# A macaron network on one core: feed-forward, norm and keys of three chunks inside the mixture of experts ahead of them, constant rows in two halves, transfers issued by SP

## The chip, the core and the metric

The kernel runs on one core of a Trainium2 chip. A core has five engines that run at the same time, each through its own instruction stream in order: PE (matrix products into PSUM), DVE (elementwise work and reductions), ACT (activation functions and copies), POOL (GpSimd), and SP, which here only issues transfers between HBM and the on-chip memory SBUF. An engine waits for another through semaphores. The metric is the device time of one execution in microseconds: 4069.91 us before the change, the median of three runs (4068.77 to 4074.88).

## What is computed

The input x has 2048 rows of 128 numbers. Blocks are added to it one after another; each reads a layer norm of x:

```python
x = x + 0.5 * L0_ffn(ln(x)); x = x + L0_attn(ln(x)); x = x + 0.5 * L0_ffn(ln(x))
x = x + 0.5 * L1_ffn(ln(x))        # first mixture of gated experts
x = x + L1_attn(ln(x))             # a long convolution
x = x + 0.5 * L1_ffn(ln(x))        # second mixture of gated experts
x = x + 0.5 * L2_ffn(ln(x))        # silu(x Wg) * (x Wu), then Wd; 384 hidden
x = x + L2_attn(ln(x))             # 16 heads of 8, rotary positions, no mask
x = x + 0.5 * L2_ffn(ln(x)); x = x + 0.5 * L3_ffn(ln(x))
x = x + L3_attn(ln(x))             # 16 heads, rotary, causal
x = x + 0.5 * L3_ffn(ln(x))
```

L1_ffn scores 8 experts for each row, keeps the two best with softmax weights, and adds the experts' outputs, each `(silu(x W1) * (x W2)) W3`. L3_ffn is a gated attention of 16 heads followed by a sparse mixture of 8 experts. Everything is in 32-bit floats, and a 32-bit product takes two passes on PE, which the trace lists as two matmuls.

## The kernel before

**Tiles.** x stays in SBUF as 16 tiles of 128 rows, and four of these (512 rows) make a chunk; there are four chunks, 0 to 3. A chunk is transposed (xnT, 128x512) to be the operand of products.

**The mixtures (`l1_ffn`, L526).** The norms of all four chunks are made first (`normed`), with the gate's logits (pl) and the choice of two experts (`top2`). Then a loop over chunks and experts makes, in two halves hb, two products h of 512 columns, Silu of the first on ACT (L554) and the product of both on DVE (L555, `hid`), and then 16 matmuls po with W3; four DVE operations (L563) add po, times the gate, to x. Every PE matmul goes through `mm`, whose line is L75, and every DVE operation of the helper `vec` has line L83. PSUM has eight banks: two for norms and logits, two each for the two h and for po.

**Order.** The kernel is written for a framework whose scheduler places the instructions of each engine by an estimate of when their inputs are ready, earlier text first. Instructions that are "pinned" keep the order of the text on their engine: on PE where `order["pinned"]` is set, on DVE, for `vec`, in the modes "core" and "drain". The mode names the phase: "free" outside the attentions, "fill" at an attention's beginning until its first product for weights, "core", and "drain" once all its scores are made.

**Between the second mixture and the first attention.** `head_buffers` (L1408) makes the tiles kp (keys of all heads), qps (four query tiles) and va (values). Each head's rows of kp and qp stand beside constant rows of zeros and ones, which are copied from a table `rest` in HBM (L1416, L1421) by SP. kp lies in memory that the mixtures' weights hold until then. After that, for chunks 0, 1, 2: `l2_chunk` (norm, transposes xn_tp, products gu with Wg and Wu, Silu, po with Wd, x updated) and `rope2.prepare` (norm again, transposes, keys: products pj, two DVE operations with the tables cos and sin, a sum on POOL, a rounded part hi on ACT and the rest lo on POOL). `send` writes hi and lo to HBM (dk for keys, dq for queries, L694), and `load_keys` brings the keys back to kp in the order of heads (L713): eight transfers a chunk in two halves of heads, of which an attention's first units need the first. Chunk 0 makes its queries too. Chunk 3 is carried into the attention as a guest.

**The attention (`attend`, L856).** A unit is a chunk of queries and a group of four heads. Scores (sn, L886) go to a maximum per row on DVE (h_mx); a unit's maxima become rows of its query tile; LAG (four) steps after, its weights (st, then Exp on ACT, pr) and outputs (av) begin. The first unit takes its keys chunk by chunk. Beside each step two guests advance by a stage: the carried chunk 3, and values and further queries. `begin` (L865) loads a unit's queries from dq into a query tile (L871). There are four attentions: L2 (rope2), gated, L3 (rope3), gated. Before the third the sparse experts run, and rope3 makes chunks 0 to 2 in "free" mode as each chunk's output is ready.

**The norm (`norm`, L177).** Statistics by bn_stats and bn_aggr, then `inv_sqrt` (L161): an estimate from integer operations and three Newton rounds, all small DVE operations of 128x4, and then one scaling for each tile, on ACT with `on_act`, else on DVE. `put` and `evac` copy PSUM to SBUF, ACT and DVE in turn except in "fill" (ACT) and "drain" (DVE). `queue` gives SP and ACT in turn in "free" and "fill", else SP.

Of the kernel before, what the change touches and what calls it, by code (L numbers as in the profile page):

```python
# [21 lines left out]
P = 128  # L22
# [20 lines left out]
def tile_macaron(ctx: ExitStack, tc: tile.TileContext, a: dict, out: bass.AP):  # L43
# [34 lines left out]
    class Ordered:  # L78
        def __getattr__(self, name):
            method = getattr(nc.vector, name)  # L80

            def call(*args, **kw):
                ins = method(*args, **kw)  # L83
                if order["mode"] in ("core", "drain"):
                    tc.keep_in_program_order(ins)
                return ins

            return call
# [3 lines left out]
    def transpose(dst, src):  # L92
        pin(nc.tensor.transpose(dst, src, ident))  # L93

# [66 lines left out]
    def inv_sqrt(pool, var, shape, tag):  # L161
# [3 lines left out]
        vec.tensor_single_scalar(g, v.bitcast(I32), 1, op=ALU.logical_shift_right)  # L165
        vec.tensor_scalar(g, g, -1.0, float(0x5F3759DF), ALU.mult, ALU.add)
        r = pool.tile(shape, F32, tag=tag + "_r", name=tag + "_r")
        prev = g.bitcast(F32)
        for _ in range(3):
            h = pool.tile(shape, F32, tag=tag + "_h", name=tag + "_h")  # L170
            vec.tensor_tensor(h, prev, prev, ALU.mult)
            vec.scalar_tensor_tensor(h, h, -0.5, v, ALU.mult, ALU.mult)
            vec.scalar_tensor_tensor(r, h, 1.5, prev, ALU.add, ALU.mult)
# [3 lines left out]
    def norm(src, dst, on_act=False):  # L177
# [5 lines left out]
        rstd = inv_sqrt(small, mv[:, :, 1], [P, TC], "ln")  # L183
        if on_act:
            nb = small.tile([P, TC], F32, tag="ln_nb", name="ln_nb")
            vec.scalar_tensor_tensor(nb, mv[:, :, 0], -1.0, rstd, ALU.mult, ALU.mult)
# [339 lines left out]
    def l1_ffn(w):  # L526
        HB = 2
        with ExitStack() as es:
            sb1 = es.enter_context(tc.tile_pool(name="m1", bufs=1))
            sb = es.enter_context(tc.tile_pool(name="m", bufs=3))  # L530
            psum = es.enter_context(tc.tile_pool(name="m_ps", bufs=2, space=PSUM))
            _, xnT = normed(psum)
            pl = psum.tile([P, NT, E], F32, tag="tp", name="pl")
            for i in range(NT):
                mm(pl[:, i, :], xnT[:, i * P : (i + 1) * P], w["l1_gT"])
            logits = sb1.tile([P, NT, E], F32, name="logits")
            nc.vector.tensor_copy(logits, pl)
# [6 lines left out]
            nc.vector.tensor_scalar_mul(gate, gate, 0.5)  # L544
            for c in range(NC):
                xc = xnT[:, c * CW : (c + 1) * CW]
                for e in range(E):
                    hid = sb.tile([P, HB, CW], F32, tag="hid", name="hid")
                    for hb in range(HB):
                        p_1 = psum.tile([P, CW], F32, tag="h1", name="h1")  # L550
                        p_2 = psum.tile([P, CW], F32, tag="h2", name="h2")
                        mm(p_1, w["l1_w12T"][:, e, hb * P : (hb + 1) * P], xc)
                        mm(p_2, w["l1_w12T"][:, e, (HB + hb) * P : (HB + hb + 1) * P], xc)
                        nc.scalar.activation(hid[:, hb, :], p_1, AF.Silu)  # L554
                        nc.vector.tensor_tensor(hid[:, hb, :], hid[:, hb, :], p_2, ALU.mult)  # L555
                    po = psum.tile([P, TC, D], F32, tag="po", name="po")
                    for t in range(TC):
                        for hb in range(HB):
                            mm(po[:, t, :], hid[:, hb, t * P : (t + 1) * P], w["l1_w3T"][:, e, hb, :],
                               start=hb == 0, stop=hb == HB - 1)  # L560
                    for t in range(TC):
                        i = c * TC + t
                        nc.vector.scalar_tensor_tensor(  # L563
                            x[:, i, :], po[:, t, :], gate[:, i, e : e + 1], x[:, i, :], ALU.mult, ALU.add
                        )
# [15 lines left out]
    pools = {}  # L581

    def ring(name, tag="w", shape=(P, CW), bufs=10):
        return pools["ring"].tile(list(shape), F32, tag=tag, name=name, bufs=bufs)
# [3 lines left out]

    def banks(name):
        return pools["sc"].tile([P, 2, CW], F32, tag="sc", name=name)  # L590
# [9 lines left out]
    def put(dst, src):  # L600
        if order["mode"] == "drain":
            vec.tensor_copy(dst, src)
        elif order["mode"] == "fill":
            nc.scalar.copy(dst, src)
        else:
            evac(dst, src)

    def queue():
        turn["q"] += 1
        return nc.scalar if order["mode"] in ("free", "fill") and turn["q"] % 2 else nc.sync  # L610
# [23 lines left out]
    def l2_chunk(c, w):  # L634
# [5 lines left out]
        for hb in range(HB):  # L640
# [4 lines left out]
            if order["mode"] == "free":  # L645
# [22 lines left out]
    class Heads:  # L668
# [38 lines left out]
        def load_keys(self, c, halves=(0, 1)):  # L707
# [9 lines left out]
            if 0 in halves:  # L717
                self.loaded.add(c)
# [137 lines left out]
    def attend(A, carried, follow, after=None):  # L856
# [4 lines left out]
        for c, halves in A.waiting_keys:  # L861
            A.load_keys(c, halves)
# [132 lines left out]
        if units[0] not in queries:  # L995
            begin(A, units[0])
        LAG = 4
# [8 lines left out]
        while nw < len(weights) or last:  # L1006
# [12 lines left out]
            if s and s[3] not in B.loaded:  # L1019
# [388 lines left out]
    def head_buffers(pool):  # L1408
# [4 lines left out]
        for j in range(2):  # L1413
            r = slice(j * KD + 4 * HD, (j + 1) * KD)
            for c in range(NC):
                nc.sync.dma_start(  # L1416
                    out=kp[r, :, c * CW : (c + 1) * CW].bitcast(F32),
                    in_=rest[0:n, :].unsqueeze(1).to_broadcast([n, NH // 2, CW]),
                )
            for qp in qps:  # L1420
                nc.sync.dma_start(  # L1421
                    out=qp[r, :, :].bitcast(F32), in_=rest[2 : n + 2, :].unsqueeze(1).to_broadcast([n, 2, CW])
# [150 lines left out]
```

## Time and profile before

| | value |
|---|---|
| median of three runs | 4069.91 us |
| the profiled execution: its time | 4074.4 us |
| the profiled execution: its span | 4072.6 us |
| PE matmuls, busy | 3557.4 us (87%), 29080 matmuls |
| DVE, busy | 3141.5 us (77%), 5645 instructions |
| ACT, busy | 2329.1 us (57%), 4436 instructions |
| POOL, busy | 215.0 us (5%), 262 instructions |
| mean granted clock of PE | 0.885 |

The profile records when each instruction of each engine began and ended, from the span's start. The page cuts the span into 40 slices of about 102 us; a digit is the busy share in tenths, and PEclk is the clock that PE was granted:

```profile
PE   8789898689999995899999965599997899999965
DVE  3855443579999975899999745689997799999844
ACT  1222122158888862688888722246675488888732
PEclk8889798779999997899999966668998799999966
```

Counted from 0, slices 2 to 3 and 4 to 6 hold the two mixtures, and the runs of nines from slice 8 on are the attentions. Slice 7 (713 to 814 us) lies ahead of the first attention, and slices 23 to 25 hold the sparse experts and what leads to the third. In a timeline line the columns are start, duration, engine, source line, operation, output<-inputs, shapes and count, and in brackets the idle time before it and what ended that; SPq and ACTq are transfers that SP and ACT issue.

### The profile page before, as it was taken

What the parts mean: (1) busy time and instruction counts of PE and PEld (TensorE: products, weight loads), DVE (VectorE), ACT (ScalarE), POOL (GpSimd) and SP (SyncE); (2) the same over time, 40 slices, a digit from 0 to 9 for tenths busy, and PEclk for the clock granted to TensorE, in tenths of its full rate; (3) what the DMA queues carried; (4) which work ended last, traced back from release to release, by engine and by line L of the source; (5) the groups of instructions that cost most, each with busy time, mean ns of one, the idle gap of its engine ahead of it and who ended that gap; (6) DMA issues with size and microseconds to landing.
All of it is one profiled execution on the core that took longest, in us unless ns stands there. A gap on an engine that the chain in (4) does not pass through costs nothing. (4 is left out here: it accounts for less than half of the span.)

```text
span 4072.6 us, 72035 instructions
## 1 busy us (share of the span) xinstructions
PE 3557.4 (87%) x29080; PEld 1680.4 (41%) x29080; DVE 3141.5 (77%) x5645; ACT 2329.1 (57%) x4436; POOL 215.0 (5%) x262
## 2 busy tenths in 40 slices
PE   8789898689999995899999965599997899999965
PEld 8566664333333342333333343243333333333334
DVE  3855443579999975899999745689997799999844
ACT  1222122158888862688888722246675488888732
POOL 2000000100000000000000033100000000000013
PEclk8889798779999997899999966668998799999966
DMA  2100003220000002100000022400002200000012
GB/s 71 25 1 1 1 1 87 62 63 7 10 7 10 4 13 57 50 9 9 7 10 4 9 70 77 110 20 10 10 2 62 54 10 7 10 7 7 7 42 74
DMA packets 71532, 111.91 MB, mean 27 GB/s; under 512 B 9712, under 2 KB 29920, under 8 KB 70944
## 3 DMA queue, kind: packets, MB, share of 16 engines
q1 hardware_dynamic: 57536, 77.81, 7.2%
q0 software_dynamic: 7088, 20.81, 2.1%
q10 hardware_dynamic: 6576, 8.69, 0.8%
q8 instruction: 229, 3.75, 0.4%
q14 instruction: 103, 0.84, 0.1%
HBM read 74.47 MB, written 31.75 MB: 26 GB/s over the span
## 5 line engine op out<-in xcount | busy, mean ns | idle before, releaser
L83 DVE TENSOR_REDUCE h_mx<-sn 128x2 f32<-128x1024 f32 (+1 forms) x1856 | 2206.3, 1197 | 141.4 <-PE sn L886 119.8
L942 ACT ACTIVATE pr<-st 128x512 f32<-128x512 f32 x3712 | 1972.7, 585 | 518.7 <-PE st L75 335.7
L75 PE MATMUL av<-pr,va 128*32 128x256 f32 x14592 | 1191.4, 399 | 10.9 <-ACT h_ot L971 10.9
L75 PE MATMUL st<-qp,kp 64*128 64x512 f32 x3712 | 998.4, 500 | 49.2 <-ACT pr L942 45.6
L886 PE MATMUL sn<-kp,qp 64*128 64x512 f32 (+3 forms) x3712 | 812.1, 416 | 126.6 <-DMA qp<-dq 46.1
L75 PEld LDWEIGHTS st<-qp,kp 64*128 64x128 f32 x3712 | 394.4, 188 | 818.1 <-ACT pr L942 441.8
L75 PEld LDWEIGHTS av<-pr,va 128*32 128x32 f32 x14592 | 293.1, 109 | 664.7 <-issue 626.8
L886 PEld LDWEIGHTS sn<-kp,qp 64*128 64x128 f32 x3712 | 388.7, 195 | 186.6 <-issue 99.8
L75 PE MATMUL h<-xnT,w_l_w12T 128*128 128x512 f32 x512 | 250.1, 611 | 1.7 <-DVE xnT L65 1.7
L554 ACT ACTIVATE hid<-h 128x512 f32<-128x512 f32 x128 | 76.4, 597 | 301.4 <-PE h L75 301.4
L75 PEld LDWEIGHTS po<-w_l_w3T,hid 128*128 128x128 f32 x1024 | 131.2, 193 | 69.1 <-DVE hid L555 47.2
L563 DVE SCALAR_TENSOR_TENSOR x<-po,gate,x 128x128 f32<-128x128 f32 x256 | 71.9, 344 | 100.4 <-PE po L75 100.3
L75 PE MATMUL po<-w_l_w3T,hid 128*128 128x128 f32 x1024 | 139.9, 279 | 1.3 <-DVE hid L555 1.3
L555 DVE TENSOR_TENSOR hid<-hid,h 128x512 f32<-128x512 f32 x128 | 87.2, 683 | 55.1 <-PE h L75 55.1
L75 PEld LDWEIGHTS h<-xnT,w_l_w12T 128*128 128x128 f32 x512 | 90.2, 197 | 66.1 <-issue 62.6
L1270 POOL DMA_INDIRECT wt<-in_b_wt,w_row_i x30 | 28.8, 960 | 1436.6 <-DVE slot_i L83 1395.0
L915 ACT CAST h_mT<-mt_ps 8x512 fp32r<-8x512 f32 x64 | 36.9, 576 | 100.4 <-PE mt_ps L93 100.2
L83 DVE BATCH_NORM_STATS2 st<-ph 128x6 f32<-128x256 f32 x46 | 19.9, 432 | 87.0 <-PE ph L75 87.0
L223 POOL TENSOR_TENSOR x<-x,w_b_n2b 128x512 f32<-128x512 f32 x8 | 10.1, 1266 | 1301.1 <-DVE rows L83 1133.7
L93 PE MATMUL xn_tp<-ident,xn_t 128*128 128x128 f32 x64 | 20.1, 406 | 66.3 <-ACT xn_t L189 62.7
L83 DVE TENSOR_TENSOR sn<-sn,mask_qk 128x256 f32<-128x256 f32 x128 | 54.2, 426 | 30.7 <-PE sn L886 29.3
L83 DVE TENSOR_TENSOR st<-st,mask_kq 128x128 f32<-128x128 f32 x256 | 63.3, 291 | 14.0 <-PE st L75 13.4
(391 smaller groups left out, 2627.5 us busy)
## 6 DMA issues: line engine op xcount, KB each, us to landing
qp<-dq SPq DMA_DIRECT2D x128, 136.0 KB
kp<-dk SPq DMA_DIRECT2D x128, 128.0 KB
dq<-hi SPq DMA_DIRECT2D x23, 256.0 KB
dq<-lo SPq DMA_DIRECT2D x23, 256.0 KB
wt<-in_b_wt SPq DMA_DIRECT2D x16, 258.0 KB
kp<-rest SPq DMA_DIRECT2D x8, 512.0 KB
dk<-lo SPq DMA_DIRECT2D x16, 256.0 KB
qp<-h_mT SPq DMA_DIRECT2D x256, 4.0 KB
```

Source lines behind the costliest of these rows:

```text
L75: pin(nc.tensor.matmul(dst, lhsT=lhsT, rhs=rhs, start=start, stop=stop))
L83: ins = method(*args, **kw)
L93: pin(nc.tensor.transpose(dst, src, ident))
L223: nc.gpsimd.tensor_tensor(xs, xs, row.unsqueeze(1).to_broadcast([P, TC, D]), ALU.add)
L554: nc.scalar.activation(hid[:, hb, :], p_1, AF.Silu)
L555: nc.vector.tensor_tensor(hid[:, hb, :], hid[:, hb, :], p_2, ALU.mult)
L563: nc.vector.scalar_tensor_tensor(x[:, i, :], po[:, t, :], gate[:, i, e : e + 1], x[:, i, :], ALU.mult, ALU.add)
L886: pin(nc.tensor.matmul(sc[:, j, :wd], lhsT=qp[r, p, t * P : (t + 1) * P], rhs=kp[r, 2 * g + p, kc * CW : kc * CW + wd], start=True, stop=True,
L915: nc.scalar.copy(mT, pt)
L942: nc.scalar.activation(pr[:, off:CW], sc[:, off:], AF.Exp, scale=A.scale)
L1270: nc.gpsimd.indirect_dma_start(wts[k], None, a["b3_wt"], bass.IndirectOffsetOnAxis(ap=w_row_i[:, s - E : s - E + 1], axis=0),)
```

## The change

1. `l1_ffn` takes a list of tasks. Its norms and logits get a PSUM pool of their own, closed before the pool of h and po opens. The expert loop is written out in two stages: `first` (h, Silu, product) yields after each half hb, and `second` (po, and the update of x) of the expert before follows after the first half of the next. For the second mixture the tasks are `l2_chunk` and `rope2.prepare` of chunks 0, 1 and 2. Chunk c's task begins when the last expert has updated chunk c, and a stage of it is written after each half of the experts of chunk c+1. There the mode is "host": PE and DVE are pinned, po has one bank, and three banks serve the guests, which so take gu in two separate banks. Chunk 3 stays a guest of the attention.
2. In "host" and "fill" a norm with its scaling on ACT makes its Newton rounds on POOL (12 operations and two for the offset in place of ten of DVE). For all norms the integer estimate takes one operation in place of two.
3. The constant rows come in two halves: those of the first query tile and the first half of heads in `head_buffers`, the others inside `attend` of rope2. `attend` now calls `begin` for its first unit ahead of the keys, and loads all chunks' first halves, then the other rows, then second halves; a score waits only for the half that it reads.
4. `put` uses ACT in every mode but "drain", and `queue` always gives SP. xnT moves to a pool that lasts, and the pools of the L2 and L3 weights open earlier.

The diff, cut to its core ("..." stands for lines left out):

```diff
     def inv_sqrt(pool, var, shape, tag, on_pool=False):
...
-        vec.tensor_single_scalar(g, v.bitcast(I32), 1, op=ALU.logical_shift_right)
-        vec.tensor_scalar(g, g, -1.0, float(0x5F3759DF), ALU.mult, ALU.add)
+        vec.tensor_scalar(g, v.bitcast(I32), -0.5, float(0x5F3759DF), ALU.mult, ALU.add)
...
+            if on_pool:
+                nc.gpsimd.tensor_tensor(h, prev, prev, ALU.mult)
+                nc.gpsimd.tensor_tensor(h, h, v, ALU.mult)
+                nc.gpsimd.tensor_scalar(h, h, -0.5, 1.5, ALU.mult, ALU.add)
+                nc.gpsimd.tensor_tensor(r, h, prev, ALU.mult)
...
+        on_pool = on_act and order["mode"] in ("host", "fill")
...
+    def l1_ffn(w, tasks=()):
...
+            with tc.tile_pool(name="m_pre", bufs=2, space=PSUM) as psum:
+                _, xnT = normed(psum)
...
+            psum = es.enter_context(tc.tile_pool(name="m_ps", bufs=2, space=PSUM))
+            if tasks:
+                pools["ring"] = es.enter_context(tc.tile_pool(name="early", bufs=1))
+                pools["tp"] = es.enter_context(tc.tile_pool(name="early_ps", bufs=3, space=PSUM))
+                order["pinned"], order["mode"] = True, "host"
...
             for c in range(NC):
                 for e in range(E):
+                    for hid in first(c, e):
+                        if late:
+                            second(*late)
+                            if late[1] == E - 1 and tasks:
+                                waiting.append([n, tasks.pop(0)])
+                            late = None
+                        if waiting and waiting[0][0] <= n:
+                            later = next(waiting[0][1], None)
+                            if later is None:
+                                waiting.pop(0)
+                            else:
+                                waiting[0][0] = n + later
+                        n += 1
+                    late = (c, e, hid)
+            second(*late)
...
     def banks(name):
+        if order["mode"] == "host":
+            return TwoBanks(name)
...
     def queue():
-        turn["q"] += 1
-        return nc.scalar if order["mode"] in ("free", "fill") and turn["q"] % 2 else nc.sync
+        return nc.sync
...
         A.current = True
-        for c, halves in A.waiting_keys:
-            A.load_keys(c, halves)
...
         if units[0] not in queries:
             begin(A, units[0])
+        for h in range(2):
+            for c, halves in A.waiting_keys:
+                if h in halves:
+                    A.load_keys(c, (h,))
+            if h == 0 and A is rope2:
+                other_rows()
...
-            if s and s[3] not in B.loaded:
+            if s and (s[3], s[1][1] // 2) not in B.loaded:
...
+        constant_rows(qps[0:1], slice(0, 4))
         nc.gpsimd.memset(va_flat, 1.0)
-        return kp, va_flat, qps
+        return kp, va_flat, qps, lambda: constant_rows(qps[1:], slice(4, 8))
...
-            l1_ffn(w1)
+            rope2, rope3 = RopeHeads("l2", w2, False), RopeHeads("l3", w3, True)
+            l1_ffn(w1, [chain([l2_chunk(c, w2), rope2.prepare(c)]) for c in range(NC - 1)])
...
-    for c in range(NC - 1):
-        finish_all([l2_chunk(c, w2), rope2.prepare(c)])
```

## The prediction

> **What bounds the kernel now.** I read first how busy each engine is by stage (windows), then the order of time around the seams, then the waits of SP. The columns of the first view are the stretch, its length, and busy time with count for PE, weight loads, DVE, ACT and POOL, then the granted clock, the DMA share and GB/s.
>
> ```profile
> 496.00:664.00 168.00, 167.37 (x759) 103.61 (x758) 82.55 (x227) 39.79 (x65) 0.00 (x0) 0.98 0.00 1
> 664.00:750.00 86.00, 52.62 (x159) 27.80 (x157) 31.60 (x152) 19.87 (x43) 13.83 (x10) 0.76 0.59 135
> 750.00:821.00 71.00, 37.74 (x121) 18.82 (x120) 39.55 (x59) 5.85 (x11) 8.44 (x9) 0.69 0.26 67
> 821.00:851.00 30.00, 23.17 (x44) 8.12 (x44) 19.50 (x22) 3.00 (x4) 7.12 (x8) 0.50 0.46 124
> 851.00:1500.00 649.00, 640.02 (x5993) 244.82 (x5992) 616.36 (x631) 546.49 (x1014) 2.52 (x2) 0.99 0.03 9
> 2548.00:2574.00 26.00, 0.44 (x1) 0.28 (x1) 4.69 (x16) 2.26 (x5) 4.89 (x5) 0.50 0.67 144
> ```
>
> The second mixture (496 to 664) and the attention (851 on) are full on PE. Between them lie 187 us in which no engine is, at a clock of 0.5 to 0.76: chunks 0 to 2 one after another, then chunk 3 beside the first scores. A second hole, at 2548, is before the third attention. The order of time says what ends each:
>
> ```profile
> 658.81 2.74 PE L75 MATMUL h<-xnT,w_l_w12T 128*128 128x512 f32 x6
> 659.01 1.13 DVE L563 SCALAR_TENSOR_TENSOR x<-po,gate,x 128x128 f32<-128x128 f32 x4 [1.92 <-PE po L75]
> 664.37 1.80 SPq L1416 DMA_DIRECT2D kp<-rest  x4
> 685.44 2.42 ACT L189 ACTIVATE xn_t<-x,ln_nb,ln_r 128x128 f32<-128x128 f32 x6 [8.19 <-DVE ln_nb L83]
> 692.64 0.75 DVE L83 SCALAR_TENSOR_TENSOR rot<-pj,w_l_bcol,cos 128x512 f32<-128x512 f32 x1 [5.97 <-DMA cos<-in_l_cos]
> 750.03 0.50 PE L886 MATMUL sn<-kp,qp 64*128 64x512 f32 x2
> 821.19 0.76 PE L886 MATMUL sn<-kp,qp 64*128 64x512 f32 x1 [12.88 <-DMA kp<-dk]
> ...
> 2552.37 15.29 SPq L713 DMA_DIRECT2D kp<-dk  x19
> 2568.21 11.34 SPq L871 DMA_DIRECT2D qp<-dq  x8
> 2573.51 0.44 PE L886 MATMUL sn<-kp,qp 64*128 64x128 f32 x1 [28.16 <-DMA qp<-dq]
> ```
>
> Constant rows (5 MB) start when the mixture's last matmul frees the memory, and hold up the tables; the first score is at 750, the fourth key chunk's at 821, the first product for weights at 851.13. At 2573 the first score waits 28 us for queries whose load stands on SP behind 19 key loads.
>
> **The guests, in PE work.** A chunk has 12 matmuls gu and 4 pj of 512 columns (0.428 us each at full clock, from six h in 2.74), 24 po (0.107 each, from 14 in 1.76) and 8 transposes (some 0.13): 6.85 + 2.57 + 1.0 = 10.4. Three chunks and the four pj of chunk 0's queries: 33 us. The mixture repeats every 5.255 us of which PE is busy 5.13, so nothing hides this: +33. It is also what leaves the stretch behind, where it took half clock.
>
> **Waits that pinning adds.** A norm's transposes are emitted two steps (one po and two h groups, 5.14 us of PE) after its statistics. DVE has the four x updates (1.15), four bn pairs (1.75) and two small operations (0.4) first: 3.3 us. Then 14 Newton operations are on POOL, then four ACT activations (1.65). No POOL operation of 128x4 is in the trace; the nearest row is
>
> ```profile
> L457 POOL COPY cz<-cT 64x1 f32<-64x1 f32 x32 | 6.0, 188 | 1.5
> ```
>
> 32 of these end 7.54 us after they start, 0.236 each; a dependent one a little more, so 0.25 and 3.5 us. The Trainium skill (GPSIMD Engine Reference, 4.1 Engine selection) speaks against the move: elementwise with two inputs is about 2 times slower than on VectorE. DVE's Newton steps here follow at 0.195, so the rule would give 0.39 and 5.5 us, 2 us more per norm and 12 over six. I take the row, since at four elements the fixed part decides, and keep 12 for the range. Then 3.3 + 3.5 + 1.65 less 5.14, and crossings between engines of 0.1, leave a stall of about 2.9; behind it on PE stand the next h matmuls, for which ACT and DVE wait. Six norms (two a chunk): +17.
>
> The clock: around 664 PE was almost idle for 4.3 us, and gu then ran at 0.95 for 5.3 us before the 0.43 came back, a loss of 2.6. The same skill (TensorE: Matmul & The Clock Gate, Why this matters for your kernels) wants no idle gap over about 3 us. By the row six gaps cost 16, by the rule those of 2.9 cost 0; I take 8. On DVE the mixture's hid product can stand behind a guest's product or a wait for tables: +3 (0 to 15). Guests' transfers: two tables (POOL queue, 0.57 + 0.54 to issue), two sends of keys, for chunk 0 four of queries, at 256 KB; the mixture moves 1 GB/s, so DMA hides them. On SP they must stand ahead of the constant rows, which wait there from 494 to the mixture's end; were one behind, its keys would go late, as in the first rival below. POOL is empty in the mixture.
>
> **Ramps.** The mixture's PSUM pool now opens after the one for its norms, so the first h waits for the copy of logits. At 506.4 the kernel before had done 18 h and 32 po of its experts inside the ramp, 11.1 us of work, as if it had begun at 495.3. Without them DVE's norms end some 2 us sooner, and logits at about 494. Even, but for a cold clock: +1 each, +2 for two mixtures (-2 to +10). A Newton chain loses one operation (0.2 us); six layernorms before this point: -3.
>
> The mixture's last matmul moves from 664.2 by 33 + 17 + 8 + 3 + 2 - 3 = 60, to **724** (bounds +30 to +110).
>
> **From there to the first weights.** Ahead of the first score now stand 2 MB of key rows and 0.25 of query rows, queries 0.27 and a chunk's half of keys 0.5: 3.0 MB. In 28 us from 664.4 the 5.25 MB up to the first table landed, 187 GB/s, so 16 us and some latency: +19. Chunk 3's own chain needs no key: norm by 9, feed-forward (12.8 from xc to x in the trace, and Tanh's extra product) by 23, norm by 31, projections and rope by 40. Its sends on SP stand behind the other rows and second halves, 8.3 MB in all, so to about 46, landed 48, keys 52. DVE has 24 reductions of the first three chunks (1.15 each, 28 us, and some 7 of others) from 19 on, so up to 54. The fourth chunk's scores at about +57, where the trace has 157; then 30 us as before (821 to 851, eight steps of scores with queries between, unchanged): +87, and 3 for order. I choose **+90**. If guest and scores keep the present order, the 71 us from first score to fourth chunk stay: 19 + 71 + 30, +118 to +120. DVE alone has 64 us of work after the first score or beside it: not under +75.
>
> First weights: 724 + 90 = 814 for 851, **-37**. From there the attention is full on PE as before and moves with it.
>
> **The third attention.** The changed order asks for the first queries before the keys, and for all first halves before second ones. Its first score is causal and needs one chunk's half. Those dk landed at 2525 and dq at 2533; DVE is free of norms from 2553.2 and idle 23.4 us. The end cannot move more than that; PE would still pass chunk 2's projection first. I take **-18** (0 to -23). What is late next: DVE's score chain, then second halves, 2 MB or 14 us at 144 GB/s, wanted by the third unit some 20 us in.
>
> **The rest.** A send on SP costs 0.53 us as on ACT; two more in a row make dq 1.1 later, hidden while keys load. Copies of PSUM move from DVE to ACT where ACT is 84% busy and DVE 95%: a few of 0.6 us, 0 (-4 to +4). Newton on POOL in the fill of other attentions, some 1.5 us a chain, lies beside scores. Experts and tails: two or three exposed 0.2: -1.
>
> Sum: -37 - 18 - 1 = -56. The durations are of a profiled run with span 4072.6 and time 4074.4; the median is 4069.9, 0.1% lower, and the difference is taken from it: **4014 us**.
>
> **Rivals.**
> - *The fill keeps its old order, or DMA holds it* (25%). SP's backlog of 8.3 MB speaks for it; chunk 3's chain needing no keys against. +120: 4044.
> - *Scores of the third attention start no earlier* (12%), since PE's order may put them behind the other chunks. The wait names qp, against it: 4032.
> - *Guests stall the mixture and the kernel is slower* (15%). PE and DVE are in program order there, so each guest wait blocks the experts too. Before, chunk 0 took 40 us from its xn_t to its sends. If PE stood idle through three such chains, the end would be 664 + 120 + 2 = 786, the first weights 876, and with -19 later: 4076; with the slow fill 4106. It decides once guests cost 116 in place of 60: beyond 33 of work, 1.9 us a step over 44 steps. PE's present idle of 33 us in 664 to 750 speaks against.
> - *Guests wait less than I think and chunk 3 goes quickly* (8%): stalls and clock at 8, fill +80: 4014 - 20 - 10 = 3984.
>
> The forecast has 40%, within 3998 to 4032. With bounds and rivals, and some 10% left out at each end, the range is 3984 to 4070. This kernel can be told from no change at about 0.2%, 8 us: faster 0.82, same 0.05, slower 0.13.
>
> **What would show it.** Guests right: gu matmuls at 0.43 in the mixture, and six PE gaps of near 3 us before xn_tp; wrong: gaps at gu or po, or h at 0.85. Seam right: first score 19 us after the last po of the mixture, first st at +90. Third attention right: qp loads ahead of second-half key loads, no PE wait of 28 us. Wrong as a whole, if first weights come after 851.

## The result, and the profile after

The changed kernel takes 4088.23 us (median of five runs, 4082.42 to 4090.73) against 4069.91 (five runs, 4065.96 to 4074.88): 1.0044 times as long, 95% interval 1.0029 to 1.0058. It is 18 us slower. The profiled execution took 4088.2 us, its span is 4086.4 (before 4072.6), the mean granted clock 0.883 (0.885).

The stages again, in the view of windows, with the columns as in the prediction:

```profile
503.00:737.00 234.00, 218.91 (x915) 131.54 (x916) 107.63 (x288) 61.79 (x110) 35.13 (x103) 0.95 0.07 21
737.00:762.00 25.00, 5.96 (x31) 5.31 (x29) 4.58 (x17) 2.23 (x5) 6.35 (x17) 0.69 0.79 162
762.00:842.00 80.00, 40.47 (x100) 18.77 (x100) 35.52 (x44) 4.64 (x9) 7.63 (x19) 0.56 0.50 95
842.00:870.00 28.00, 19.60 (x46) 7.14 (x46) 19.39 (x22) 3.00 (x4) 7.12 (x8) 0.69 0.40 124
870.00:1500.00 630.00, 621.41 (x5914) 236.92 (x5913) 607.69 (x615) 537.11 (x997) 2.53 (x2) 0.99 0.03 9
```

The mixture holds the guests now, and PE is busy for 94% of it (before 99.6%). Behind it the seam (the stretch from the mixture's last matmul to the first weights) has shrunk from 187 us to 133, not to 90. The stretch from the first score to the fourth chunk's, in which PE had none of the work that has moved, was 71 us and has grown to 80, at a clock of 0.56 (before 0.69). The order of time in the changed kernel:

```profile
557.05 1.49 PE L93 MATMUL xn_tp<-ident,xn_t 128*128 128x128 f32 x4 [2.06 <-ACT xn_t L203]
...
736.80 0.50 PE L75 MATMUL po<-w_l_w3T,hid 128*128 128x128 f32 x3
...
748.31 0.58 ACT L661 COPY xc<-xn_tp 128x512 f32<-128x512 f32 x1 [1.76 <-PE xn_tp L93]
...
762.20 1.99 PE L937 MATMUL sn<-kp,qp 64*128 64x512 f32 x4 [12.22 <-DMA kp<-dk]
...
771.96 2.04 PE L75 MATMUL gu<-xc,l_wgT 128*128 128x512 f32 x2 [0.43 <-DVE h_mx L83]
...
825.44 0.54 SPq L748 DMA_DIRECT2D dk<-hi  x1
...
830.86 10.92 SPq L767 DMA_DIRECT2D kp<-dk  x8
...
842.56 1.98 PE L937 MATMUL sn<-kp,qp 64*128 64x512 f32 x4 [20.59 <-DMA kp<-dk]
...
869.98 0.50 PE L75 MATMUL st<-qp,kp 64*128 64x512 f32 x2
```

Read the third and fifth lines together. Chunk 3's feed-forward had its operand xc at 748.9 and PE was idle, yet its first product gu ran at 772: it stands on PE behind sixteen score matmuls (eight reductions of DVE), and the first of these waits for keys until 762.2. From there gu, po and transposes alternate with scores that DVE reduces one by one. The chunk's keys leave at 825, their loads take 10.9 us to issue in place of 3.6, and the fourth chunk's first score waits 20.6 us for them. In the kernel before, the same eight loads were:

```profile
817.28 3.62 SPq L713 DMA_DIRECT2D kp<-dk  x8
```

Offsets against the kernel before, matmul by matmul of the same count: first weights 18.8 us late, 17.7 through the first attention, 25.5 through the second, 11.0 after the start of the third, 13.8 at the end.

In the third attention the first score runs at 2569.8, where before it ran at 2573.5, but the next ones wait (order of time, PE):

```profile
2569.77 0.33 PE L937 MATMUL sn<-kp,qp 64*128 64x128 f32 x1
2580.80 0.66 PE L937 MATMUL sn<-kp,qp 64*128 64x128 f32 x3 [10.71 <-DMA qp<-dq]
...
2604.12 0.44 PE L937 MATMUL sn<-kp,qp 64*128 64x128 f32 x1 [15.06 <-DMA qp<-dq]
```

The wait of 28 us for qp has become two, of 10.7 and 15.1, for the second transfer of the first unit and for the next unit's.

### The profile page after: what moved, and what is told of

It reads as the page before. It is cut to its first block, busy times and chain, and to the rows that moved or that the text cites. A ratio compares the mean times of both kernels' runs of the same rounds, so it can differ in the third digit from the quotient of the medians.

```text
span 4086.4 us, 72030 instructions
## 1 busy us (share of the span) xinstructions
PE 3557.8 (87%) x29080; PEld 1691.3 (41%) x29080; DVE 3112.2 (76%) x5422; ACT 2331.5 (57%) x4443; POOL 257.9 (6%) x466
## 5 line engine op out<-in xcount | busy, mean ns | idle before, releaser
L75 PE MATMUL av<-pr,va 128*32 128x256 f32 x14592 | 1187.8, 398 | 10.6 <-ACT h_ot L1022 10.5
L575 ACT ACTIVATE hid<-h 128x512 f32<-128x512 f32 x128 | 76.2, 597 | 241.7 <-PE h L75 239.5
L75 PE MATMUL po<-w_l_w3T,hid 128*128 128x128 f32 x1024 | 126.4, 275 | 2.1 <-DVE hid L83 2.1
L237 POOL TENSOR_TENSOR x<-x,w_b_n2b 128x512 f32<-128x512 f32 x8 | 10.1, 1268 | 1125.5 <-DVE rows L83 1122.0
L93 PE MATMUL xn_tp<-ident,xn_t 128*128 128x128 f32 x64 | 20.6, 382 | 66.7 <-ACT xn_t L203 62.8
```

The costliest lines, as they stand in the source:

```text
L75: pin(nc.tensor.matmul(dst, lhsT=lhsT, rhs=rhs, start=start, stop=stop))
L237: nc.gpsimd.tensor_tensor(xs, xs, row.unsqueeze(1).to_broadcast([P, TC, D]), ALU.add)
```

## Experiments

Every time stands beside runs of the kernel before on the same chip, and the ratio is to those. "Behind the mixture" counts from the last po of the second mixture in that kernel's trace. A trace is of one execution, which lies up to 14 us from its kernel's median (4051.9 for 4066.2 with the query loads split), so the traces tell where time goes and the medians how much. Where two kernels ran on different chips, on which the kernel before took between 4066.0 and 4070.3, the difference of their ratios stands beside that of their times.

### What the guests and the order of loads are worth

The guests taken out, the rest of the change kept:

```diff
-            l1_ffn(w1, [chain([l2_chunk(c, w2), rope2.prepare(c)]) for c in range(NC - 1)])
+            l1_ffn(w1)
...
+    for c in range(NC - 1):
+        finish_all([l2_chunk(c, w2), rope2.prepare(c)])
```

> The changed kernel, but the feed-forward, norm and keys of chunks 0 to 2 stand between the mixture and the attention again, as in the kernel before; halves, order of loads, SP and the norms' reciprocal roots on GpSimd stay. Theory (the guests themselves pay nothing, because the seam behind them keeps its old order): the mixture ends at about 672 in the trace (8 us later than before, from the two ramps), the first weights near 865, the third attention keeps its gain of 14, the second attention its loss of 7; time about 4071, so the guests with their old seam cost some 17. Rival (the guests save their 37 us and the other parts lose it): the time is over 4115.

Measured: 4089.25 us, ratio 1.0060 (1.0039 to 1.0080). The mixture ends at 673.7, first weights at 873.6, 199.8 behind it. So the guests add 63.6 us to the mixture, take 67.1 from the seam, and bring nothing that the time can tell (4089 and 4088). Both accounts of mine missed: not the guests but the other parts lose 20 us. About 10 are there when the mixture ends, and 13 come in a seam that should have been the old one. Of these 13, 7 are key loads that take 10.7 us to issue behind two loads of queries, where they took 3.6 (more on this below); the rest is there at the first score (92.5 behind the mixture for 85.8), and what causes it was not separated.

Then the kernel before with nothing but the first queries ahead of the keys, and first halves ahead of second ones:

```diff
-        for c, halves in A.waiting_keys:
-            A.load_keys(c, halves)
...
             begin(A, units[0])
+        for h in range(2):
+            for c, halves in A.waiting_keys:
+                if h in halves:
+                    A.load_keys(c, (h,))
```

> The kernel before with one part of the change alone: an attention's first queries are loaded ahead of the keys, and all first halves of keys ahead of the second. Theory (this part alone gives the third attention's gain): first score of the third attention about 28 us earlier on its wait for qp, the attention done 14 us earlier, time about 4055. Rival (the gain came from the norms or the copies moved to other engines): the end of that attention moves by under 5, time 4065 or more.

Measured: 4062.79 us, ratio 0.9988 (0.9972 to 1.0005), which doesn't tell a gain; by the interval it is at most 11 us. In the trace the offset to the kernel before goes from -8.3 to -28 within the third attention's start, where the changed kernel gained 14.5. That shows the place, but those 20 us are more than the times allow, and this execution was 11 us faster than its median: how much this part is worth stays open. At the first attention this order costs nothing (186.2 us from the mixture to the first weights, before 186.9).

### The order at the seam

Chunk 3 emitted as a whole ahead of the first score; the scheduler still places it, but earlier text goes first:

```diff
+        if A is rope2:
+            order["mode"] = "fill"
+            finish_all(carried)
+            carried = []
         LAG = 4
```

> The changed kernel with chunk 3's feed-forward, norm and keys emitted as a whole ahead of the first attention's first score. Theory (the order of TensorE holds the seam: chunk 3's first product stood 23 us behind eight scores that waited for keys, and then ran between scores): the last dk is sent at about 785 in place of 826, the first scores start near 780 in place of 762, the first weights near 830 in place of 870; time about 4048, 40 below the changed kernel. Rival (transfers hold the seam, 8 MB on SP): keys of chunk 3 land no earlier than about 830, first weights not before 855, time over 4073.

Measured: 4047.68 us, ratio 0.9953 (0.9938 to 0.9968), where the order's account asked for 4048. That it fits so closely is luck: in this trace the last keys leave and the first weights come some 10 us later than that account said. The rival, that transfers hold the seam, had first weights not before 855. The mixture ends at 741.7:

```profile
751.24 2.07 PE L75 MATMUL gu<-xc,l_wgT 128*128 128x512 f32 x2 [0.68 <-ACT xc L661]
...
794.75 0.54 SPq L748 DMA_DIRECT2D dk<-hi  x1
...
839.55 0.97 PE L75 MATMUL st<-qp,kp 64*128 64x512 f32 x2 [3.79 <-DMA qp<-h_mT]
```

gu follows its operand, the keys leave 53 us behind the mixture in place of 88, and first weights come at 97.9 in place of 132.7, though the first score came 12 us later than in the changed kernel (37.2 for 24.9). The place of one chunk in the written order is worth some 40 us (37 by the ratios). The edit moves the chunk ahead on every engine; that PE's stream is what held it is read from gu's wait behind the scores, above.

The same order without guests:

> Chunk 3 first and no guests: chunks 0 to 2 between mixture and attention, one after another, then chunk 3, then the scores. Theory (guests cost in the mixture nearly what they save behind it, about 65 for 75): mixture ends near 674, first scores 112 behind it, first weights 172 behind it, so near 846; time 4050 to 4060. Rival (the guests' full gain shows once the order is right, 37 us as forecast): first weights at 875 or later, time 4080 or more.

Measured: 4069.92 us, ratio 1.0013 (1.0001 to 1.0024); first scores 121.4 and first weights 185.1 behind the mixture, not 112 and 172. So guests are worth 22 us with chunk 3 first (4069.9 to 4047.7; 24 by the ratios), where they take 87 out of the seam (185.1 to 97.9) for 64 in the mixture, and nothing in the old order, where they take 67.

One finer cut, made on the best of the versions below: only the feed-forward ahead, norm and keys beside the scores.

> As the run before, but only chunk 3's feed-forward ahead of the scores; its norm and keys run beside them again. Theory (DVE's reductions hold the seam once the feed-forward is out of the way, so a first score near 29 in place of 35 is worth some 6 us): first weights about 91 after the mixture, time 5 below the run before. Rival (scores ahead of the chain delay chunk 3's keys again): first weights over 105, time 8 or more above it.

Measured: 4022.92 us, ratio 0.9893 (0.9862 to 0.9923), against 4027.89 without this edit, with intervals that overlap. First weights came 105.4 behind the mixture, later than the 103.0 beside it, so a gain, if any, doesn't come from the seam. This stays open.

### The pauses that pinning adds

```diff
-        yield 2
+        yield 3 if order["mode"] == "host" else 2
```

> The changed kernel with a guest's transposes one step of the mixture later (three behind its norm in place of two). Theory (six stalls of 2.1 us, transposes paced by the activations, 0.37 us each in place of 0.13, and after each a 3.4 us window at half clock): no TensorE gap before xn_tp, h at 0.43 throughout, the mixture ends near 712 in place of 737, time about 4065. Rival (the pause is only moved, since the last chunk's guest then ends behind the mixture): the end moves by less than 10, time over 4078.

Measured: 4080.99 us, ratio 1.0025 (1.0011 to 1.0040). The mixture is 13.9 us shorter (first h to last po 220.2 for 234.1), not 25. PE waits at xn_tp only 0.35 us in the three norms where nothing else stalls, and four h behind it take 1.88 us, as at full clock. But the other three norms stall elsewhere. ACT, DVE and PE in this kernel, in the order of time:

```profile
716.45 1.65 ACT L203 ACTIVATE xn_t<-x,ln_nb,ln_r 128x128 f32<-128x128 f32 x4 [5.38 <-POOL ln_nb L198]
718.00 0.57 ACT L575 ACTIVATE hid<-h 128x512 f32<-128x512 f32 x1
...
718.61 0.69 DVE L83 TENSOR_TENSOR hid<-hid,h 128x512 f32<-128x512 f32 x1 [4.37 <-ACT hid L575]
...
719.35 2.88 PE L75 MATMUL po<-w_l_w3T,hid 128*128 128x128 f32 x14 [4.33 <-DVE hid L83]
```

ACT reaches the guest's scaling before the experts' Silu and waits there 5.4 us for POOL's last operation; Silu, hid and po wait behind it. The stall has moved from PE's order to ACT's. Of the 14 us some 9 reach the first weights, which come 137.3 behind the mixture in place of 132.7: the last guest's keys now leave 6 us behind it.

Beside the three edits of the next group the same edit brought nothing:

> The run before with a guest's transposes one step later. Theory (the last guest's keys then leave 8 us after the mixture, but the first score waits for chunk 3's chain until about 35 anyway, so that the 14 us saved inside the mixture stay): mixture end 14 earlier, first weights 10 to 14 earlier, time 10 to 12 below the run before. Rival (as without chunk 3 first, where 14 in the mixture were 7 in the time): at most 5.

Measured: 4027.89 us, ratio 0.9890 (0.9864 to 0.9916), against 4028.19. First weights are only 3.4 us earlier (819.9 for 823.3).

### Ramps and reciprocal roots

The mixtures' PSUM tiles laid out ahead of the norms again, the guests' three banks shared with the norms (with chunk 3 first):

```diff
-            with tc.tile_pool(name="m_pre", bufs=2, space=PSUM) as psum:
-                _, xnT = normed(psum)
+            psum = es.enter_context(tc.tile_pool(name="m_ps", bufs=2, space=PSUM))
+            pre = es.enter_context(tc.tile_pool(name="early_ps", bufs=3 if tasks else 2, space=PSUM))
+            _, xnT = normed(pre)
```

> Chunk 3 first, as in the run before, and the mixtures' PSUM tiles laid out ahead of their norms again (norms and guests share three banks), so that the experts can start on the first chunk while others are normed. Theory (the two ramps cost about 8 us, in place of the 2 forecast): the first h of both mixtures comes before the copy of logits, the end of the second mixture is 8 us earlier than with chunk 3 first alone, time about 4040. Rival (the ramp is DVE's norms, and the order of pools moves nothing): under 2 us.

Measured: 4043.15 us, ratio 0.9946 (0.9928 to 0.9964), 4.5 below 4047.68 with overlapping intervals, so no gain is told from the time. Over all traces of this study the first mixture's share is plain: it ends at 419.8 to 429.9 (mean 426.0) in eight kernels with the old layout, at 431.3 to 438.5 (mean 434.6) in ten with the new one. For the second they leave it open: from the first's last po to its own it takes 239.5 us without guests, where the kernel before took 234.7, but with guests 302 to 303 with the new layout and 301 to 305 with the old.

The roots of norms in the fill back on DVE (with chunk 3 first):

```diff
-        on_pool = on_act and order["mode"] in ("host", "fill")
+        on_pool = on_act and order["mode"] == "host"
```

> Chunk 3 first, and the reciprocal roots of norms in the fill back on DVE; guests inside the mixture keep them on GpSimd. Theory (a chain on GpSimd is 3.9 us for 2.2 on DVE, and in the fill a norm is waited for): first weights about 4 us after the mixture's end earlier (94 for 97.9), the second attention's first weights lose 4 in place of 8 against the kernel before, time about 4040. Rival (the loss at the second attention is the half clock after a longer pause, not the chain): its loss stays at 7 to 9 and the time within 3 of 4047.

Measured: 4045.81 us, ratio 0.9946 (0.9931 to 0.9960). Half right: first weights unchanged (98.2 behind the mixture for 97.9), because the keys leave at 53 either way, held by loads on SP; but at the second attention the offset to the kernel before goes from -21.5 to -25, where with chunk 3 first alone it went from -14 to -5.5. The time shows only 2 of the 12; single traces differ by as much as 10 in places that an edit doesn't touch.

All three together:

> Chunk 3 first, the mixtures' old ramp, and the fill's reciprocal roots on DVE, together. Theory (each was worth 2 to 12 us alone: ramps 5 to 8, roots 2 to 12 at the second attention): time 4030 to 4040, against 4048 with chunk 3 first alone; the second attention's first weights lose nothing against the kernel before. Rival (run to run differences of 10 us have been read as gains): within 3 of 4045.

Measured: 4028.19 us, ratio 0.9895 (0.9870 to 0.9920). And ramps and roots without chunk 3 first:

> The changed kernel in its own order (chunk 3 beside the scores), with the old ramp of the mixtures and the fill's roots on DVE. Theory (the parts add up: together they were worth 19 with chunk 3 first): time 4066 to 4072, no faster than the kernel before, so that without a new order at the seam the guests bring nothing. Rival (ramps and roots are the whole failure): first weights under 840, time under 4050.

Measured: 4064.28 us, ratio 1.0003 (0.9987 to 1.0019): 24 us below the changed kernel (17 by the ratios) and level with the kernel before, with first weights 129.9 behind the mixture. With chunk 3 first the two bring 19 (24 by the ratios). So ramps and roots account for some 17 to 24 us in either order, and alone they win nothing against the kernel before.

### Which transfer waits for which

Sends of the fill in turn on ACT's queue and SP again, with chunk 3 first and then in the changed kernel's own order:

```diff
     def queue():
-        return nc.sync
+        turn["q"] = turn.get("q", 0) + 1
+        return nc.scalar if order["mode"] in ("free", "fill") and turn["q"] % 2 else nc.sync
```

> Chunk 3 first, and sends of the fill alternate between ACT's queue and SP again. Theory A (sends stand behind SP's backlog of loads): chunk 3's first dk leaves at about 45 us after the mixture in place of 53, first weights 5 to 8 us earlier, time about 4041. Theory B (DVE's 32 reductions and the rotations between them fill the time from the first score to the first weights): dk earlier, first weights unchanged within 2, time within 3 of 4047.

> The changed kernel with one part undone: sends of the fill alternate between ACT's queue and SP. Theory (sends by SP alone cost nothing as the sum had it; loads that come behind chunk 3's send in the shared order are its own keys, so nothing new stands behind ACT's send): time within 5 of 4088, first weights within 3 of 870. Rival (SP alone is part of the loss at the seam): first weights 5 or more earlier, time under 4080.

Measured: 4081.37 us, ratio 1.0030 (1.0017 to 1.0043), and 4103.33 us, ratio 1.0086 (1.0061 to 1.0111). All theories fell: two queues cost 34 and 15 us (31 and 17 by the ratios). With chunk 3 first its keys did leave earlier, 38 us behind the mixture for 53, but first weights came at 128.5 for 97.9. In the own order only 7 us of the loss are in the seam (139.4 for 132.7); the rest comes later and was not followed up. The longest lines of SP's waits, first with chunk 3 first, then in the own order (us in total, times, longest):

```profile
SPq L768 <- DMA dk<-hi: 21.7, 1, 21.7
```

```profile
SPq L768 <- DMA dk<-hi: 47.2, 1, 47.2
```

A load of other chunks' keys waits on SP for chunk 3's send on ACT, of which it needs nothing. The instructions of these kernels say why: a transfer is told as landed by one of eight semaphores, taken in turn by SP's and ACT's transfers together, and it is not issued before the last one with the same semaphore has landed. A load eight places behind a send waits until that send has landed, on whatever queue. "All transfers issued by SP" was no loss but a saving.

In the changed kernel one slow transfer does the same: of its seam, SP's waits put 17.6 us of key loads down to qp<-dq. So the second unit's queries were put behind chunk 3's keys, with PE's order unchanged:

```diff
+            if A is rope2 and A.scored < 13:
+                k = len(units)
             if k < len(units) and units[k] not in queries and units[k][0] in A.sent:
...
+                        if self.pre == "l2":
+                            tc.keep_in_program_order(ins)
...
+                if u[0] == 0 and A is rope2:
+                    tc.keep_in_program_order(ins)
```

> The changed kernel with the query rows of the first attention's second unit loaded behind chunk 3's keys and not ahead of them; TensorE's order is the same. Theory (eight transfers are under way at most, and every eighth waits for a query load that lands slowly: chunk 3's key loads took 10.9 us to issue in place of 3.6): they issue in 4 to 7 us, the fourth chunk's first score waits 14 to 17 us in place of 20.6, first weights 4 to 7 earlier, time 4081 to 4084. Rival (tables and memory bandwidth, not the queries, slow these loads): issue still over 9 us, first weights within 2.

Measured: 4079.97 us, ratio 1.0032 (1.0018 to 1.0046), 8 us below the changed kernel (5 by the ratios), first weights 123.1 behind the mixture, for 132.7. The order of time on SP:

```profile
825.83 0.52 SPq L748 DMA_DIRECT2D dk<-lo  x1
829.83 3.62 SPq L767 DMA_DIRECT2D kp<-dk  x8
```

The same eight loads issue in 3.62 us and not 10.92. Two loads of queries, 136 KB each, held up a megabyte of keys. Why they land so slowly is in the last windows before those keys landed in the changed kernel (columns as above):

```profile
840.00:842.00 2.00, 0.00 (x0) 0.00 (x0) 0.00 (x0) 0.00 (x0) 0.00 (x0) 0.50 0.13 38
```

Nothing computes, and the 16 DMA engines are busy to 0.13, which is 2 of 16. The rule that fits is quoted in the expectation; the edit makes 34 rows into 32 and 2:

```diff
-                nc.sync.dma_start(
-                    out=qp[j * KD : j * KD + KR + 2, :, :].bitcast(F32),
-                    in_=rows_of(dq[qc], j)[:, 2 * g : 2 * g + 2, :],
-                )
+                for r0, r1 in ((0, KR), (KR, KR + 2)):
+                    nc.sync.dma_start(
+                        out=qp[j * KD + r0 : j * KD + r1, :, :].bitcast(F32),
+                        in_=rows_of(dq[qc], j)[r0:r1, 2 * g : 2 * g + 2, :],
+                    )
```

> The changed kernel with one edit: the load of a unit's query rows, 34 rows at once, is made of one of 32 rows and one of 2. The Trainium skill (DMA: Bandwidth & Descriptors, Why a DMA increments its semaphore by 16 and not by 1) says that a transfer is spread over as many of 16 engines as divide its slowest dimension; by it 34 rows go over 2, and 32 over 16, and the trace has a DMA share of 0.13, 2 in 16, while the rest of such a load is awaited. Theory (the load's spread makes it slow): chunk 3's key loads issue in under 6 us behind the queries, first score 4 or more earlier behind the mixture (20 for 24.9), first weights 7 to 10 earlier, the third attention's waits for qp of 10.7 and 15.1 shrink by half; time 4068 to 4076. Rival (the queries wait for their own dq or for bandwidth): no landing earlier, and with twice the transfers time 4088 or more.

Measured: 4066.15 us, ratio 1.0000 (0.9988 to 1.0012): 22 us below the changed kernel (18 by the ratios) from one edit, with the same order of matmuls on PE in the seam. The semaphores' events in the two traces bear the theory out: a load of 34 rows raises its semaphore twice as data land, the last time 7.0 to 15.9 us after its issue (six loads of the seam), and one of 32 rows sixteen times, the last after 3.1 to 8.0 us. The order of time on SP in its seam:

```profile
743.59 10.55 SPq L767 DMA_DIRECT2D kp<-dk  x12
...
818.51 3.63 SPq L767 DMA_DIRECT2D kp<-dk  x8
```

The twelve first loads took 17.90 us to issue in the changed kernel. First score 18.5 behind the mixture, first weights 118.1 (14.6 earlier). Another 9 us are gained at the first attention's end, where the next attention's first scores wait for their queries; first the changed kernel, then this one:

```profile
1563.34 0.76 PE L937 MATMUL sn<-kp,qp 64*128 64x512 f32 x1 [12.97 <-issue]
1566.76 0.76 PE L937 MATMUL sn<-kp,qp 64*128 64x512 f32 x1 [2.66 <-DMA qp<-dq]
```

```profile
1540.84 1.52 PE L938 MATMUL sn<-kp,qp 64*128 64x512 f32 x2 [7.42 <-DMA qp<-dq]
```

The third attention's start gains 19 in place of 14.5, but its waits for qp are 10.1 and 13.2, not the half: there the theory missed. In the trace the next unit's queries are issued on SP behind twenty loads of keys, which take 12.95 us; another order wasn't tried. In the version that was fastest so far:

> The same edit in the kernel with chunk 3 first, the old ramp and the roots on DVE (4028). Theory: at the first seam DVE's reductions hide the loads, so 0 to 4 there; the third attention's first weights 10 earlier; time 4014 to 4020. Rival (hidden everywhere): within 4 of 4028.

Measured: 4008.86 us, ratio 0.9859 (0.9837 to 0.9880), 59 us below the kernel before beside it (4067.52) and 19 below the version without the split (15 by the ratios). First weights come 88.8 behind the mixture, which is the forecast 90; DVE did not hide the loads, and 8 us came there (96.8 to 88.8); 9 more came at the first attention's end, as above. Ramps, roots and split loads without chunk 3's new place were not run together; if the parts add up (an estimate from the ratios 1.0044, 1.0003 and 1.0000) that kernel too would be some 17 us faster than the one before. Most of its seam, 12 to 70 us behind the mixture, in the view of windows:

```profile
746.00:803.00 57.00, 38.36 (x132) 18.90 (x130) 42.12 (x62) 4.66 (x9) 8.65 (x10) 0.73 0.97 183
```

DMA is busy to 0.97 and moves 183 GB/s, where the changed kernel's 762 to 842 had 0.50 and 95: here the transfers themselves fill the stretch.

## Why the prediction was wrong, step by step

| step, us | forecast | measured |
|---|---|---|
| guests in the mixture (33 + 17 + 8 + 3) | 61 | 63.6 |
| two ramps and the shorter estimate of roots | -1 | 9.5 |
| mixture's end, against before | +60 | +73.1 |
| from there to the first weights | 90 | 132.7 |
| first weights, against before | -37 | +18.8 |
| second attention | 0 | +7.8 |
| third attention | -18 | -14.5 |
| the rest | -1 | +1.7 |
| span | -56 | +13.8 |

**The step that failed** is "Chunk 3's own chain needs no key: norm by 9, feed-forward ... by 23 ..." and with it "+90". Every time in it is what the chain takes alone, with chunk 3 ahead of the scores. In that order the runs come near its sum (97.9 with chunk 3 first, 88.8 with faster loads besides), though not by its route: the first score then comes at 37.2 and 33.8, not at 19. But that a chain needs no key does not put it ahead of instructions that do. PE runs one stream whose order is fixed before the run, the diff left chunk 3's place in the text alone, and the trace of before showed what comes of that place: 71 us from the first score to the fourth chunk's. I took the data's order for the engine's. Of the 42.7 us by which the seam was over the forecast, the order makes 34.8 (132.7 to 97.9) and the spread of the query loads 8 more (96.8 to 88.8). The first rival had the mechanism ("The fill keeps its old order, or DMA holds it") and was given 25%; it should have been the forecast. With the query loads split the old order takes 118.1, within its +118 to +120. Its 4044 was 44 too low: some 40 by what follows, and the rest because the medians differ by 18.3 where the two traced spans differ by 13.8.

**The guests** were priced well in sum, by the route that was shown. Six gaps before xn_tp of 2.03 to 2.17 us make 12.5; in addition the 24 transposes took 8.25 us, where 0.13 each makes 3.1, as they follow ACT's four scalings; together 17.6 for 17. That is luck in part: as written, 3.3 + 3.5 + 1.65 less 5.14 leave 3.3 for each norm, and not 2.9. POOL's operations are 0.28 us apart (0.25 by the forecast's row, 0.39 by the rule beside it), so the row was the better guide. The clock took more than the quoted rule allowed:

```profile
556.90:558.70 1.80, 1.48 (x5) 0.78 (x6) 0.00 (x0) 1.38 (x5) 1.05 (x2) 1.00 0.27 89
558.70:562.10 3.40, 3.40 (x5) 1.35 (x4) 0.35 (x1) 1.05 (x2) 0.00 (x0) 0.50 0.29 107
562.10:565.50 3.40, 3.40 (x11) 1.61 (x10) 1.03 (x3) 1.19 (x2) 0.00 (x0) 0.99 0.00 0
```

After the gap of 2.06 us came 3.4 us at half clock, and h took 0.82 each; six times some 1.6 us make 10, for 8. (33, 17.6 and 10 make 60.6 of the 63.6 measured; the other 3 were not traced.) The rule that the prediction quotes (the Trainium skill, TensorE: Matmul & The Clock Gate, Why this matters for your kernels) wants no idle gap over about 3 us. The gap here is 2.06, but the four transposes behind it, spread over 1.49 us, leave PE little to do either. The kernel with transposes one step later separates the two: there a bare pause of 2.55 us is followed by half clock too, and a pause of 0.35 us ahead of transposes as widely spread (1.48 us) is not:

```profile
590.53 3.28 PE L75 MATMUL po<-w_l_w3T,hid 128*128 128x128 f32 x14 [2.55 <-DVE hid L83]
```

```profile
590.20:593.60 3.40, 3.07 (x14) 3.07 (x15) 0.88 (x2) 0.04 (x1) 0.43 (x1) 0.50 0.00 0
```

```profile
555.85 1.48 PE L93 MATMUL xn_tp<-ident,xn_t 128*128 128x128 f32 x4 [0.37 <-ACT xn_t L203]
```

```profile
558.80:562.20 3.40, 3.40 (x21) 2.55 (x20) 1.81 (x5) 0.49 (x2) 0.00 (x0) 1.00 0.01 5
```

**The ramps** were mis-sized: 2 for both, where the first mixture alone ends 8.6 us later in the mean of the traces (4.5 in the two that the table compares). The sum let the second mixture's experts lose nothing if the logits are copied at 494, as DVE's norms end sooner. Counted from the first mixture's end, the norms' last small operation on DVE does end 3.1 us sooner (59.8 for 62.9), but the copy of the logits only 0.2 (69.1 for 69.4), and the first h stands behind it, at 69.2, where the sum needed 65.8. That makes 3.4 of the 4.8 us that the second mixture lost without guests (239.5 for 234.7); the other 1.4 would fit a start with an empty pipeline, which no run shows.

**"Newton on POOL in the fill ... lies beside scores"** is wrong. At the second attention's start a norm is the last thing before its keys, and nothing lies beside it. First before, then after (DVE or POOL, and ACT):

```profile
1627.61 0.16 DVE L83 TENSOR_TENSOR ln_h<-ln_g 128x4 f32<-128x4 f32 x1
...
1629.58 1.65 ACT L189 ACTIVATE rows<-x,ln_nb,ln_r 128x128 f32<-128x128 f32 x4 [13.03 <-DVE ln_nb L83]
```

```profile
1650.38 0.20 POOL L175 TENSOR_TENSOR ln_h<-ln_g 128x4 f32<-128x4 f32 x1 [39.94 <-DVE ln_g L83]
...
1654.26 1.65 ACT L203 ACTIVATE rows<-x,ln_nb,ln_r 128x128 f32<-128x128 f32 x4 [15.79 <-POOL ln_nb L198]
```

From the first Newton operation to the scaling it is 1.97 us on DVE and 3.88 on POOL. Most of the rest of the 7.8 is clock: PE waits 8.07 and 7.32 us for the scalings in place of 6.31 and 5.72, and between them four pairs of gu took 2.08, 1.71, 2.08 and 1.54 us where they had taken 1.13, 1.02, 1.13 and 1.02. With the roots back on DVE the loss is gone, with and without chunk 3 first. From the last weights of the first attention to the first of the second the offset rises by 3.7 to 10.5 us in the ten kernels with roots on POOL, and by -3.2 to 4.1 in the seven others with them on DVE. The kernel with only its query loads split is one of the ten, at 9.5, though the 9 us it gains just ahead of that stretch hide it.

**The third attention** came close (14.5 for 18). Alone that part gave 20 in its trace and at most 11 by its times, so the size is not settled. The forecast's "late next: DVE's score chain, then second halves" was wrong in kind: the queries are late again.

**DMA** was judged by bytes. 3.0 MB ahead of the first score at 187 GB/s gave +19; it was 24.9, and 18.5 with the queries spread over more engines, so the 19 held once the loads were spread.

## What to carry to other kernels

Before counting what work a change takes out of a stretch, ask what each engine's written order does with what is left: a chain that depends on nothing still waits behind an instruction that does, and moving work away pays only when the rest may move up. Price a transfer by how many engines it is spread over and by what shares its completion semaphores, not by its bytes alone. Cover for a moved operation must be named at every place where it runs, the last one before a wait among them.

## What the runs showed of the hardware that was not expected

- A load of 34 rows (136 KB) kept about 2 of 16 DMA engines busy (share 0.13, 38 GB/s); split into 32 and 2 rows it made two kernels 22 and 19 us faster (18 and 15 by the ratios). The Trainium skill (DMA: Bandwidth & Descriptors, Why a DMA increments its semaphore by 16 and not by 1) states the rule by which 34 rows go to 2 engines.
- Transfers on two queues are not independent in these kernels: with eight completion semaphores in common, a key load on SP stood 47 us behind a send on ACT's queue.
- A bare pause of 2.55 us in PE's work was followed by 3.4 us at half clock, and so were pauses of 2.03 to 2.17 us with thin work behind them.
- A dependent 128x4 operation follows the last at 0.28 us on POOL and at 0.20 on DVE.
